# A transformer block on one core: charges and router tokens turned by way of memory, second statistics on ScalarE, a new order

## The chip, the cores and the metric

The kernel runs on one core of a Trainium2 chip. The metric is the device time of one execution in microseconds. A core has five engines that run side by side, each through its own instructions in a fixed order: TensorE (PE; its weight loads are PEld), VectorE (DVE), ScalarE (ACT), GpSimd (POOL) and SyncE (SP), which here issues nearly all transfers between memory (DRAM) and the on-chip buffer (SBUF). TensorE writes its results to PSUM, eight banks of 128 x 512 numbers.

## What is computed

The input x has 32 sequences of 512 tokens with 256 numbers each, all in float32. The reference adds two blocks to it:

```python
x = x + attn(layernorm(x))
x = x + ffn(layernorm(x))
# attn, per sequence
q = tanh(x @ W_charge.T + b_charge)[..., 0]            # one number per token
shell = normalise(x @ W_shell.T + b_shell)             # 64
proj = shell @ omega.T + rff_bias
phi_s = concat([cos(proj), sin(proj)]) * rff_scale     # 64
phi = (mags * q**[0..4] outer phi_s) @ W_combine.T     # 64
attn = softmax(causal(phi @ phi.T * decay / temp))
out = (attn @ (x @ W_v.T + b_v)) @ W_out.T + b_out
# ffn, per sequence
h = gelu([x, mean of slots] @ w1.T + b1)               # 128
alpha = softmax over the 8 largest of (h @ w2.T + b2) / (|tau| + 0.1)   # 64 slots
slots = GRU(alpha.T @ x / sum(alpha), slots)
out = (alpha @ (slots @ wv.T + bv)) @ wo.T + bo
```

## The kernel before, in words

Two sequences form a group (`GB = 2`, 1024 tokens, eight tiles of 128 tokens); 16 groups follow each other, and several are in work at once. A group goes through these stages; names are those of the tiles in the profile:

1. Load: `x` (token by partition), and, from the third group on, `xb`, the same numbers loaded a second time from DRAM in blocks of 32 x 32, so that VectorE's 32 x 32 transposes (L876) give `xT`, the tokens turned so that the feature is the partition. The first two groups turn on TensorE instead (L854). `xb` has two buffers.
2. First statistics (`bna`, L786, `lna` on POOL), and `pf = xT @ [W_shell, W_charge, W_v W_out]` (L906); VectorE scales it and adds the bias into `sv` (L919).
3. Charges: POOL repeats each token's charge 64 times (`qrep`, L945), TensorE turns this (`ptq`, L965), ScalarE takes tanh and the square into `qs` (L975, L983). Beside it the shells are normalised (`sq`, `rn`, `shn`), turned and projected (`pts`, `pp`); angles are rounded (`turn`), and a sine gives `tp`'s first power. VectorE makes the four others by two products with `qs` (L1099).
4. `pph` combines the powers to `phi` (L1111, L1126).
5. Attention in three pieces per sequence: logits `pl` (L1165), mask and row minimum `lg`, `nm` (L1194, VectorE), exponentials `pr` (L1206, ScalarE), turned on TensorE and copied (`ptp`, L1243; `prT`, L1261), values `po` (L1249), and the residual addition into `x` (L1278, VectorE).
6. Second statistics: `bnb` (L786, VectorE), ten small operations on POOL (`lnb`, L797 to L807), and `xm`, the normalised tokens (L1301, ScalarE). TensorE turns them (`ptb`, L822), ScalarE copies them to `xmT` (L834).
7. Router: `ph` (L1328), gelu `h_t`, `prr`, turned to `prt`, `rl`; the eight largest by `top` and `rest` (L1384, L1385), weights `al` (L1418, POOL).
8. Slots: `psi` (L1442), copied to `gi` (L1456, VectorE), GRU (`prz`, `pn`, `rz`, `nn`, `rh`, `hn`), values `pv`, outputs `py` (L1600), added to `x` (L1614, VectorE) and stored by SP (L1619).

The order of each engine's instructions is worked out by a planner in the file when the program is built (`Plan.order`). Each step is added with its engine, a cost, the steps it needs, the tiles it uses and, for a transfer, a time to landing. The planner places the step that can start first, ties going to the lower rank; a rank is the group's number times `STRIDE` plus the step's place in its group plus a `DELAY` of its stage. It also knows how many buffers each kind of tile has (`SLOTS_OF`) and holds a step back until one is free. An engine then carries out its list strictly in order: an instruction that waits holds up all behind it, on SP too.

Of the kernel before, what the change touches and what calls it, by code (L numbers as in the profile page):

```python
# [11 lines left out]
AF = mybir.ActivationFunctionType  # L12
# [12 lines left out]
BY_TENSOR = 2  # L25
SHELL = 64
# [30 lines left out]
    "xT": 4,  # L57
    "xmT": 4,
# [9 lines left out]
    "row": 7,  # L68
    "half": 4,
# [3 lines left out]
HOP = 0.41  # L73
TABLE = 1.28
SWITCH = 1.77
STRIDE = 26.98
LATE = 0.0
# [3 lines left out]
    "load": (4.9, -6.0),  # L81
    "tokens": (10.7, 1.0),
    "angles": (-1.4, -34.3),
    "phi": (3.9, 0.9),
    "weights": (-3.0, 1.9),
    "values": (17.8, -4.4),
    "normal": (17.2, 16.3),
    "router": (34.1, 12.7),
    "taken": (-19.4, 7.1),
    "gru": (-29.8, 4.8),  # L90
    "given": (20.5, 17.4),
# [152 lines left out]
def block_kernel(ctx: ExitStack, tc: tile.TileContext, a: dict, out: bass.AP):  # L244
# [11 lines left out]
    def lazy(tag, name, shape, dtype=F32):  # L256

        if tag not in pools:
            kind = {"space": bass.MemoryType.PSUM} if tag == "ps" else {}
            pools[tag] = ctx.enter_context(  # L260
                tc.tile_pool(name=f"{tag}_pool", bufs=SLOTS_OF.setdefault(tag, 1), **kind)
            )
        return Lazy(tag, lambda: pools[tag].tile(shape, dtype, tag=tag, name=name))
# [87 lines left out]
    w1x = const("w1x", [P, KD, H])  # L351
    b1e = const("b1e", [H, 1])
# [324 lines left out]
    l_w1x = load("SP", w1x, rows(a["w1_t"][0:D, :]), 128, rank=30.0)  # L677
    l_w1s = load("SP", w1s, rows(a["w1_t"][D : 2 * D, :]), 128, rank=30.0)
# [99 lines left out]
    def statistics(g, n, src, uses, after):  # L778

        st = small(f"bn{n}_{g}", [P, GT, 6])  # L780
        ts = small(f"ln{n}_{g}", [P, 5, GT])
# [11 lines left out]
        def spread():  # L793

            mean, rs, dm, va, nmr = (ts()[:, k, :] for k in range(5))
# [8 lines left out]
            if n == "b":  # L804
                ev.tensor_tensor(mean, st_[:, :, 1], st_[:, :, 4], ALU.add)
                ev.tensor_tensor(nmr, mean, rs, ALU.mult)
                ev.tensor_scalar(nmr, nmr, -0.5, None, ALU.mult)  # L807

        s = add("POOL", 3.3 if n == "a" else 4.1, spread, ss + [s_ones], [st, ts])
        return ts, s  # L810

    def transposed(g, n, src, uses, after, tag):

        res = {}
        for bb in range(GB):
            for k in range(KD):
                pt = bank(f"pt{n}_{g}_{bb}_{k}")
                dst = lazy(tag, f"{tag}_{g}_{bb}_{k}", [P, T])

                def turn(bb=bb, k=k, pt=pt):  # L820
                    for c in range(NT):
                        nc.tensor.transpose(  # L822
                            pt()[:, c * P : (c + 1) * P],
                            src()[:, bb * NT + c, k * P : (k + 1) * P],
                            ident,
                        )

                s = add(
                    "PE", 0.47, turn, after[bb * NT : (bb + 1) * NT] + [s_ident], uses + [pt, dst]
                )  # L830
                s = add(
                    "ACT",
                    0.54,
                    lambda dst=dst, pt=pt: nc.scalar.copy(dst(), pt()),  # L834
                    [s],
                    [pt, dst],
                )
                res[bb, k] = (dst, s)
        return res
# [49 lines left out]
    def features(g):  # L889
# [6 lines left out]
        ln, s_ln = statistics(g, "a", xt, [xt], arrived)  # L896
# [41 lines left out]
        qrep = lazy("row", f"qrep_{g}", [P, GB, NT // 2, 2, PHI_S])  # L938
# [3 lines left out]
        def repeated(bb):  # L942
            for h in range(2):
                lo = bb * NT + (h ^ bb) * (NT // 2)
                nc.gpsimd.tensor_copy(  # L945
                    qrep()[:, bb, :, h, :],
                    sv()[:, lo : lo + NT // 2, C_Q : C_Q + 1].to_broadcast([P, NT // 2, PHI_S]),
                )

        s_rep = [  # L950
            add(
                "POOL",
                0.63,
                lambda bb=bb: repeated(bb),
                s_sv[bb * NT : (bb + 1) * NT],
                [qrep, sv],
            )
            for bb in range(GB)
        ]
        ptq = bank(f"ptq_{g}")  # L960
        qs = lazy("qs", f"qs_{g}", [P, 2, T])

        def charges_turned():
            for c in range(NT):
                nc.tensor.transpose(  # L965
                    ptq()[:, c * P : (c + 1) * P],
                    qrep()[:, c // 2, c % 2].rearrange("p h s -> p (h s)"),
                    ident,
                )

        s = add("PE", 0.45, charges_turned, s_rep + [s_ident], [qrep, ptq, qs])
        s = add(
            "ACT",
            0.61,
            lambda: nc.scalar.activation(qs()[:, 0, :], ptq(), AF.Tanh),  # L975
            [s],
            [ptq, qs],
            "exp",
        )
        s_q = add(  # L980
            "ACT",
            0.62,
            lambda: nc.scalar.activation(qs()[:, 1, :], qs()[:, 0, :], AF.Square),  # L983
            [s],
            [qs],
        )

# [23 lines left out]
        def norms():  # L1011
# [7 lines left out]
                0.4,  # L1019
# [72 lines left out]
        for m in (1, 3):  # L1092

            def powers(m=m):
# [612 lines left out]
```

## Time and profile before

| | |
|---|---|
| three runs, median (lowest to highest) | 717.17 us (716.65 to 717.93) |
| profiled execution, its own time | 716.61 us |
| span from first to last instruction | 714.8 us |
| busy: PE, DVE, ACT, POOL | 686.8, 595.3, 422.5, 236.2 us |
| mean granted TensorE clock | 0.993 of full speed |
| moved by DMA | 53.76 MB, 75 GB/s over the span |

How to read the rows: a group of instructions has its line, engine, operation, the tiles written and read, shapes and count; then the busy time of all (overlaps once) and the mean duration of one in ns; then the time for which the engine stood idle just before them and who ended it. Rows of stages give the start and end of a stretch, its length, and for PE, PEld, DVE, ACT and POOL the busy time with the number of instructions, then the granted clock, the share of the 16 DMA engines in use and GB/s. A timeline row gives start, duration, engine and operation; SPq is SP's queue, where the duration of several issues is that of the whole series. A landing is the time from the issue of a transfer to the arrival of its last byte.

### The profile page before, as it was taken

The page shows a single profiled execution, that of the slowest core. Times are in us where ns is not written, and L with a number is a line of the kernel's source. Part 1 is how long each engine was busy: PE and PEld are TensorE (multiplying, and loading weights), DVE is VectorE, ACT ScalarE, POOL GpSimd, SP SyncE. Part 2 cuts the span into 40 slices and gives each one's busy share as a digit, 9 for nine tenths or more (in the row PEclk, how much of TensorE's full clock was granted, in tenths as well). Part 3 has the DMA queues.
Part 4 walks back from the last instruction along what each step waited for, and adds up shares of the span by engine and source line. Part 5 has one row for each costly group of instructions (what it writes and reads, how often), then busy time and mean ns, then how long its engine had stood idle before and what let it go on. Part 6 is the DMA issues. An engine that isn't in the chain of part 4 may idle for free.

```text
span 714.8 us, 12300 instructions
## 1 busy us (share of the span) xinstructions
PE 686.8 (96%) x4170; PEld 480.2 (67%) x4170; DVE 595.3 (83%) x1750; ACT 422.5 (59%) x867; POOL 236.2 (33%) x470
## 2 busy tenths in 40 slices
PE   3989999999999999999999999999999999999884
PEld 3757676767676766767676776767667676777453
DVE  3999888789798989979897979979899887878474
ACT  1445849585755747656565856467475655758720
POOL 3640532214334432324324133423423243321120
PEclk9999999999999999999999999999999999999989
DMA  6796113032304223331412333131330301001013
GB/s 179 161 278 121 34 26 60 2 118 58 119 2 115 63 60 118 60 120 25 94 59 60 119 60 118 27 93 60 59 118 1 118 1 60 1 1 60 0 60 118
DMA packets 100016, 53.76 MB, mean 75 GB/s; under 512 B 64017, under 2 KB 99153, under 8 KB 99953
## 3 DMA queue, kind: packets, MB, share of 16 engines
q1 hardware_dynamic: 98640, 52.45, 28.3%
q8 instruction: 33, 0.54, 0.3%
q10 hardware_dynamic: 1104, 0.36, 0.2%
q0 software_dynamic: 208, 0.17, 0.2%
q14 instruction: 31, 0.25, 0.1%
HBM read 35.85 MB, written 16.78 MB: 74 GB/s over the span
## 4 chain that ended last, share of the span: by engine, by line
PE 89%; DVE 4%; ACT 2%; DMA 2%; issue 1%; POOL 1%; DVEq 0%; ACTq 0%; POOLq 0%
PE po L1249 20%; PE pf L906 18%; PE ph L1328 7%; PE pl L1165 5%; PE pph L1111 5%; PE ptp L1243 5%; PE psi L1442 4%; PE py L1600 4%; PE ptb L822 4%; PE prz L1492 4%; PE pv L1580 2%; PE prr L1353 2%; PE pn L1492 2%; PE pta L1563 1%; DMA x<-in_x_dram 1%; PE pp L1053 1%
## 5 line engine op out<-in xcount | busy, mean ns | idle before, releaser
L1249 PE MATMUL po<-sv,prT 128*128 128x256 f32 x640 | 149.6, 380 | 0.0
L906 PE MATMUL pf<-wfb,xT 128*128 128x321 f32 x448 | 133.2, 439 | 0.0
L1249 PEld LDWEIGHTS po<-sv,prT 128*128 128x128 f32 x640 | 117.0, 189 | 22.6 <-issue 5.9
L906 PEld LDWEIGHTS pf<-wfb,xT 128*128 128x128 f32 x448 | 80.4, 190 | 37.5 <-issue 6.8
L1301 ACT ACTIVATE xm<-x,lnb 128x256 f32<-128x256 f32 x128 | 66.0, 594 | 43.3 <-POOL lnb L807 43.3
L1206 ACT ACTIVATE pr<-lg,nm 128x128 f32<-128x128 f32 (+3 forms) x128 | 70.7, 555 | 13.1 <-DVE nm L1194 9.8
L1278 DVE SCALAR_TENSOR_TENSOR x<-po,den,x 128x256 f32<-128x256 f32 x128 | 60.3, 475 | 20.3 <-PE po L1249 20.0
L945 POOL COPY qrep<-sv 128x128 f32<-128x128 f32 x64 | 17.8, 294 | 154.1 <-DVE sv L919 154.1
L919 DVE SCALAR_TENSOR_TENSOR sv<-pf,lna,bias_f 128x321 f32<-128x321 f32 x128 | 63.8, 543 | 4.3 <-PE pf L906 3.9
L1194 DVE CUSTOM_DVE_ANT_0 lg<-pl,mask 128x128 f32<-128x128 f32 (+3 forms) x128 | 55.9, 487 | 6.9 <-PE pl L1165 6.8
L1328 PE MATMUL ph<-xmT,w1x 128*128 128x512 f32 x128 | 59.5, 596 | 0.0
L786 DVE BATCH_NORM_STATS2 bnb<-x 128x6 f32<-128x256 f32 x128 | 53.3, 424 | 3.1
L1261 ACT COPY prT<-ptp 128x384 f32<-128x384 f32 (+1 forms) x96 | 45.9, 517 | 4.9 <-PE ptp L1243 4.7
L786 DVE BATCH_NORM_STATS2 bna<-x 128x6 f32<-128x256 f32 x128 | 46.9, 413 | 0.0
L1243 PE MATMUL ptp<-ident,pr 128*128 128x128 f32 x320 | 45.4, 274 | 0.4 <-ACT pr L1206 0.3
L1243 PEld LDWEIGHTS ptp<-ident,pr 128*128 128x128 f32 x320 | 37.1, 140 | 8.5 <-ACT pr L1206 2.4
L1614 DVE TENSOR_TENSOR x<-py,x 128x512 f32<-128x512 f32 x64 | 39.9, 684 | 3.3 <-PE py L1600 3.0
L834 ACT COPY xmT<-ptb 128x512 f32<-128x512 f32 x64 | 33.3, 589 | 15.8 <-PE ptb L822 15.8
L1165 PE MATMUL pl<-phi 64*128 64x256 f32 (+1 forms) x384 | 42.4, 356 | 0.0
L797 POOL TENSOR_TENSOR lnb<-bnb 128x8 f32<-128x8 f32 x16 | 9.8, 612 | 94.4 <-DVE bnb L786 94.4
L1099 DVE TENSOR_TENSOR tp<-tp,qs 128x1024 f32<-128x1024 f32 x32 | 39.4, 1231 | 1.3 <-ACT tp L1085 0.7
L876 DVE STREAM_TRANSPOSE xT<-xb 128x512 f32<-128x512 f32 x56 | 38.2, 695 | 0.5 <-issue 0.4
(171 smaller groups left out, 1291.7 us busy)
## 6 DMA issues: line engine op xcount, KB each, us to landing
x<-in_x_dram SPq DMA_DIRECT2D x32, 512.0 KB, 4.8
out_dram<-x SPq DMA_DIRECT2D x64, 256.0 KB, 2.5
xb<-in_x_dram SPq DMA_DIRECT2D x112, 128.0 KB, 3.4
setup<-in_gru_whh_t_dram SPq DMA_DIRECT2D x1, 768.0 KB, 4.6
wih<-in_gru_wih_t_dram SPq DMA_DIRECT2D x1, 768.0 KB, 7.9
wfb<-wf SPq DMA_DIRECT2D x8, 40.1 KB, 3.4
setup<-in_W_v_dram SPq DMA_DIRECT2D x1, 256.0 KB, 3.5
setup<-in_W_out_t_dram ACTq DMA_DIRECT2D x1, 256.0 KB, 9.2
```

The source lines that it names most:

```text
L786: lambda t=t: nc.vector.bn_stats(st()[:, t, :], src()[:, t, :]),
L906: nc.tensor.matmul(pf()[:, 0:NF], tile_()[:, k, c * P : (c + 1) * P], w[:, k, :], start=(k == 0), stop=(k == KD - 1),)
L919: lambda t=t, pf=pf: nc.vector.scalar_tensor_tensor(sv()[:, t, :], pf()[:, 0:NF], ln()[:, 1, t : t + 1], bias_f, ALU.mult, ALU.add,),
L1165: nc.tensor.matmul(pls[bb]()[:, off[i] + lo : off[i] + lo + w], phi()[r, 0, q : q + P], phi()[r, 1, k : k + w], start=True, stop=True,)
L1194: nc.vector.tensor_tensor_reduce(out=lg()[:, c], in0=pls[bb]()[:, c], in1=mask[:, T - w : T], scale=1.0, scalar=TOP, op0=ALU.add, op1=ALU.min,
L1206: nc.scalar.activation(pr()[:, c], lg()[:, c], AF.Exp, bias=nm(), scale=-1.0, accum_out=den()[:, tiles.index(i), bb : bb + 1],)
L1243: nc.tensor.transpose(pt()[:, j : j + P], prs[bb]()[:, j : j + P], ident)
L1249: nc.tensor.matmul(po()[:, d * D : (d + 1) * D], pr_t()[:, lo : lo + P], sv()[:, bb * NT + j, C_V:NF], start=(j == 0), stop=(j == i),)
L1261: lambda width=width, pt=pt, pr_t=pr_t: nc.scalar.copy(pr_t()[:, 0:width], pt()[:, 0:width]),
L1278: nc.vector.scalar_tensor_tensor(xt()[:, t, :], po()[:, d * D : (d + 1) * D], den()[:, d, bb : bb + 1], xt()[:, t, :], ALU.mult, ALU.add,)
L1301: lambda t=t: nc.scalar.activation(xm()[:, t, 0:D], xt()[:, t, :], AF.Identity, bias=ln()[:, 4, t : t + 1], scale=ln()[:, 1, t : t + 1],),
L1328: nc.tensor.matmul(ph(), w1x[:, k, :], tiles[k](), start=(k == 0), stop=(k == KD - 1))
```

## The change

Four things are edited at once, and the planner's constants with them, so that the order of all engines is another.

- Charges: ScalarE takes tanh and square on the 128 x 8 charges as they stand in `sv` (`qc`), SP stores these 128 x 16 numbers to a DRAM tile `qd` in the order of the tokens, and four transfers read them back, each repeated over 64 partitions, as `qs`. The copies on POOL and the turns on TensorE go.
- Router's tokens: for all groups but the last two (`LAST_BY_TENSOR = 2`), `xm` is stored to a DRAM tile `xd` (one transfer a sequence), read back in blocks of 32 x 32 by four transfers into a buffer of the kind `xb`, which keeps two buffers, and turned by two VectorE transposes a sequence. The matching rows of `w1` are loaded in that order (`w1b`).
- Second statistics: VectorE's residual addition also sums each row; POOL makes the negative mean; ScalarE squares `x` minus mean with a running sum; POOL makes the scale and shift by three operations.
- The copy of the taken tokens (`gi`) goes from VectorE to ScalarE.

```diff
-    "xT": 4,
-    "xmT": 4,
+    "xT": 3,
+    "xmT": 2,
+    "xd": 2,
...
+    "qd": 2,
-    "row": 7,
-    "half": 4,
+    "row": 6,
+    "half": 5,
-HOP = 0.41
+HOP = 0.35
-SWITCH = 1.77
-STRIDE = 26.98
-LATE = 0.0
+SWITCH = 0.45
+STRIDE = 22.33
+LATE = 1.0
 DELAY = {
...
@@ def normalised(g, xm, after):
+            if g >= NG - LAST_BY_TENSOR:
...
+            else:
+                xd = lazy("xd", f"xd_{g}_{bb}", [T, D])
+                xb = lazy("xb", f"xmb_{g}_{bb}", [P, T // SQ, KD * SQ])
                 s = add(
+                    "SP",
+                    1.0,
+                    lambda bb=bb, xd=xd: nc.sync.dma_start(
+                        out=xd().rearrange("(c p) d -> p c d", p=P),
+                        in_=xm()[:, bb * NT : (bb + 1) * NT, 0:D],
+                    ),
+                    of,
+                    [xm, xd],
+                    land=3.8,
+                )
+                for q in range(P // SQ):
+                    def back(q=q, xd=xd, xb=xb):
+                        nc.sync.dma_start(
+                            out=xb()[q * SQ : (q + 1) * SQ, :, :],
+                            in_=xd().rearrange("(t i) (q e) -> q i t e", i=SQ, q=P // SQ)[q],
+                        )
+                    s_b.append(add("SP", 0.7, back, [s], [xd, xb], land=4.0))
+                for h in range(2):
+                    def turn(h=h, n=n, dst=dst, xb=xb):
+                        nc.vector.transpose(
...
+                    done.append(add("DVE", 0.63, turn, s_b, [xb, dst]))
@@ def features(g):
+        s = add("ACT", 0.25,
+            lambda: nc.scalar.activation(qc()[:, 0, :], sv()[:, :, C_Q], AF.Tanh), s_sv, [sv, qc], "exp")
+        s = add("ACT", 0.2,
+            lambda: nc.scalar.activation(qc()[:, 1, :], qc()[:, 0, :], AF.Square), [s], [qc])
+        s = add("SP", 0.6,
+            lambda: nc.sync.dma_start(
+                out=qd().rearrange("m b (c p) -> p (m b c)", p=P),
+                in_=qc().rearrange("p m t -> p (m t)"),
+            ), [s], [qc, qd], land=3.5)
+        for h in range(2):
+            for bb in range(GB):
+                def repeated(h=h, bb=bb):
+                    lo = (h ^ bb) * HT
+                    nc.sync.dma_start(
+                        out=qs()[h * PHI_S : (h + 1) * PHI_S, :, bb, :],
+                        in_=qd()[:, bb, lo : lo + HT].partition_broadcast(PHI_S),
+                    )
+                s_q.append(add("SP", 0.6, repeated, [s], [qd, qs], land=3.0))
...
-            s_tp.append(add("DVE", 1.25, powers, [s_tp[-1], s_q], [tp, qs]))
+            s_tp.append(add("DVE", 1.25, powers, [s_tp[-1]] + s_q, [tp, qs]))
@@ def attention(g, sv, s_sv, phi, s_phi):
                             ALU.add,
+                            accum_out=ln()[:, 0, bb, i : i + 1],
@@ def router(g, s_x, ln):
-        ln, s_ln = statistics(g, "b", xt, [xt], s_x)
+        for tiles in ((0, 1), (2,), (3,)):
+            s = add("POOL", 0.25,
+                lambda c=c: nc.gpsimd.tensor_scalar(
+                    ln()[:, 2, :, c], ln()[:, 0, :, c], -1.0 / D, None, ALU.mult), ...)
+            for bb in range(GB):
+                for i in tiles:
+                    s_sq.append(add("ACT", 0.6,
+                            lambda bb=bb, i=i: nc.scalar.activation(
+                                xm()[:, bb * NT + i, 0:D],
+                                xt()[:, bb * NT + i, :],
+                                AF.Square,
+                                bias=ln()[:, 2, bb, i : i + 1],
+                                accum_out=ln()[:, 3, bb, i : i + 1],
+                            ), [s], [xm, xt, ln]))
+        def deviations():
+            nc.gpsimd.tensor_scalar(va, va, 1.0 / D, LN_EPS, ALU.mult, ALU.add)
+            nc.gpsimd.tensor_tensor(rs, va, nhalf, ALU.pow)
+            nc.gpsimd.tensor_tensor(nmr, nm, rs, ALU.mult)
...
-        xm_t = transposed(g, "b", xm, [xm], s_xm, "xmT")
+        xm_t = normalised(g, xm, s_xm)
+        w1, w1_done = (w1x, [l_w1x]) if g >= NG - LAST_BY_TENSOR else (w1b, l_w1b)
@@ def slots(g, xm, al, s_al):
-            "DVE", 0.38, lambda: nc.vector.tensor_copy(gi(), psi()[:, 0:D]), [s_psi], [psi, gi]
+            "ACT", 0.38, lambda: nc.scalar.copy(gi(), psi()[:, 0:D]), [s_psi], [psi, gi]
```

## The prediction

> **What bounds the kernel now.** I read the busy shares first, then the chain that ended last, then the table of stages over two groups in the middle (one group in its two alternating orders), then the costliest groups and the waits.
>
> ```profile
> PE 686.8 (96%) x4170; PEld 480.2 (67%) x4170; DVE 595.3 (83%) x1750; ACT 422.5 (59%) x867; POOL 236.2 (33%) x470
> ...
> PE 89%; DVE 4%; ACT 2%; DMA 2%; issue 1%; POOL 1%; DVEq 0%; ACTq 0%; POOLq 0%
> ...
> 350.39:391.56 41.17, 41.17 (x287) 28.68 (x286) 35.46 (x104) 24.93 (x52) 14.78 (x29) 1.00 0.29 78
> 391.56:433.50 41.94, 41.94 (x231) 29.50 (x230) 37.57 (x111) 26.34 (x54) 14.13 (x29) 1.00 0.31 76
> ```
>
> The stage rows give length, then PE, PEld, DVE, ACT and POOL busy. PE has no gap in 83.11 us, so a group takes 41.56 us and PE sets it. DVE is next with 73.03 / 2 = 36.5 us a group; ACT has 25.6. The clock is full (1.00), so no gain or loss hides there. Of the span, 28 us of PE idle lie in the first 58 us and the last 73 us.
>
> **The change part by part.**
>
> *TensorE.* Removed are the turns of the router's tokens (14 of 16 groups; the last two keep them) and the turns of the charges (all 16).
>
> ```profile
> L822 PE MATMUL ptb<-ident,xm 128*128 128x128 f32 x256 | 33.4, 275 | 0.0
> L965 PE MATMUL ptq<-ident,qrep 128*128 128x128 f32 x64 | 9.7, 274 | 0.0
> ```
>
> Busy time counts overlapping matmuls once, so it is the time by which PE's row gets shorter: 33.4 / 16 = 2.09 us a group and 9.7 / 16 = 0.61 us. 14 x 2.09 = 29.2 us; charges count for 15 groups, since group 0's lie in the start where PE waits anyway: 9.1 us. Sum 38.3 us. One rule of the Trainium skill speaks against reading it so: "Perfetto Trace Analysis", Identifying the Most-Contended Engine, holds matmul busy time for a bad measure, since matmuls are pipelined, and takes weight-load share instead, here 67%. If only load time counted, the two loads' rows (28.6 x 14/16 + 7.5 = 32.5 us) would go. But the stage rows show PE without a gap, and four turns advance PE by 0.52 us although each lasts 275 ns; I keep 38.3. A group then needs 41.56 - 2.70 = 38.9 us of PE.
>
> *VectorE.* It loses the second statistics and the copy of the taken tokens, and gains four transposes a group and a running sum in each residual addition.
>
> ```profile
> L1278 DVE SCALAR_TENSOR_TENSOR x<-po,den,x 128x256 f32<-128x256 f32 x128 | 60.3, 475 | 20.3 <-PE po L1249 20.0
> L786 DVE BATCH_NORM_STATS2 bnb<-x 128x6 f32<-128x256 f32 x128 | 53.3, 424 | 3.1
> L876 DVE STREAM_TRANSPOSE xT<-xb 128x512 f32<-128x512 f32 x56 | 38.2, 695 | 0.5 <-issue 0.4
> L1194 DVE DVE_READ_ACCUMULATOR2_ANT nm<- 128x1 f32 x128 | 10.7, 84 | 0.0
> L1456 DVE COPY gi<-psi 128x256 f32<-128x256 f32 x16 | 6.8, 423 | 6.8 <-PE psi L1442 6.4
> ```
>
> A group: -53.3/16 = -3.33; -6.8/16 = -0.42; +4 x 38.2/56 = +2.73 (same shape as the tokens' transposes). The running sum: "VectorE: DVE Perf Modes" (Two Vector instructions with no wait between them) says that an accumulator output makes two instructions; the read in the row of the masked minimum costs 84 ns, so 8 x 0.084 = +0.67 (between 0, if it overlaps the next instruction, and this). Sum -0.35: 36.5 -> 36.15 us a group, now 93% of PE's 38.9 instead of 88%.
>
> *ScalarE.* A group: -33.3/16 = -2.1 (copies of the turned tokens), -(9.7 + 10.2)/16 = -1.2 (charges), +0.45 for two small ones over 128x8 (nearest: 0.2 us each, the 128x1 rows), +8 squares of 128x256 with a sum (the 128x256 exponentials with their reads follow each other every 0.49 us) = +3.9, +0.4 for the taken tokens' copy. 25.6 -> 27.1 us. Not the bound; table loads stay three a group.
>
> *GpSimd.* Ten small operations of the second statistics (rows `lnb`, 72.7/16 = 4.5 us a group) become six, and the charges' copies (17.8/16 = 1.1 us) go. Nobody waits longer for it.
>
> *SyncE and DMA.* SP's queue has 14 transfers a group; 15 come in: two stores of normalised tokens (512 KB), eight loads back (128 KB), one store of charges, four loads that repeat them.
>
> ```profile
> 435.32 2.17 SPq L1619 DMA_DIRECT2D out_dram<-x  x4
> 441.45 0.93 SPq L277 DMA_DIRECT2D x<-in_x_dram  x2
> 461.40 5.85 SPq L277 DMA_DIRECT2D xb<-in_x_dram  x8
> ```
>
> Issue times: 0.54, 0.46 and 0.73 us each. SP's new total is 16 x 0.73 + 11 x 0.54 + 2 x 0.46 = 18.5 us of 38.9: not a bound by throughput. Nor are the DMA engines: 0.30 x 41.56 = 12.5 us a group now; the eight loads back cost as the eight token loads do (58% of 9 us = 5.2 us), stores and repeats (1.5 MB) about as `x` and outputs (7.3 us for 2 MB, so 5.5), charges 2 to 3: some 26 of 38.9 us. Bursts will queue behind each other, which is where latency comes from.
>
> *The new ring.* The order of the changed program's instructions is the same in every middle group. On SP: four token loads, two stores of normalised tokens, three token loads, four loads back (first sequence), the store of charges, one token load, four outputs, three repeats, four loads back (second sequence), the last repeat, `x`. The store of charges stands behind loads that wait until VectorE has emptied the one shared block buffer; the repeats wait for that store to land; the second loads back and the last repeat stand behind them; and VectorE's first product of powers (`tp`, which now waits for all four repeats) stands ahead of all its later work, hence of the transposes that empty the buffer. Once round: VectorE from the first product to the emptied buffer, by pitches in the timeline: six transposes 4.1, second product 1.2, two additions 1.1, eight first statistics 2.9, four `phi` 1.35, five gate operations 2.35, eight masked minima 3.3, eight `sv` 3.9, small ones 0.5 = 20.7 us; then four issues 2.9, charges' issue 0.7, their landing L, three repeats 1.5, four issues 2.9, one repeat 0.5, landing 3.2 (median of the token loads in the middle). Sum 32.4 + L.
>
> L is what no row shows: 2 x 8 numbers from each of 128 partitions, 2048 pieces of 4 bytes written to memory. The skill speaks against it: "DMA: Bandwidth & Descriptors", Rules for kernel authors, says that a non-contiguous last dimension becomes one descriptor per element. Lower end: 2.6 us, the landing of the scalar load `lt` (128 pieces of 4 bytes). Upper end: the charge weights (256 pieces) landed in 3.7; 1.1 us more for 128 pieces, carried on, gives 2.6 + 16.5 = 19.1 us. Nearest row: four token loads, also 2048 pieces: 3 x 0.73 + 3.2 = 5.4 us; behind the loads ahead of it about 1 us more. I take 6.4 us: ring 38.8 us, just PE's 38.9. At L = 9.2 it reaches the 41.56 of now.
>
> *Stalls.* VectorE leaves 38.9 - 36.15 = 2.75 us a group. Its waits for ACT and POOL now (turn 7.2, top 6.0, rh 2.0 and smaller, 19.5 us in all) are 1.2 us a group and stay. New are two waits for loads back and one for repeats, on a queue that is in order. I charge each load 0.95 us (half the spread from 2.4 to 4.3 us of the token loads' landing in the middle), the repeats 0.3, since their ring just closes. 1.2 + 1.9 + 0.3 = 3.4, 0.65 above what is free. While DVE stands there, `sv`, masked minima and additions come late, and PE with them. 14 groups x 0.65 = 9.1 us.
>
> Start and end: group 0's powers need the charges at 43.2 us and have them at 31.6 now; through memory they take some 11 us more, just covered (uncovered 1 to 3 us). In the tail the statistics lose four small POOL operations and get two squares: nothing.
>
> Sum against the profiled execution, 716.6 us (span 714.8 and 1.8 around it): 716.6 - 38.3 + 9.1 = 687.4. The median of the runs lies 0.6 above: 688 us.
>
> **Rivals.**
> - *PE stays without gaps* (landing early enough everywhere, as the DMA engines' free time would allow): 717.2 - 38.3 = 679 us. Against it: 93% of DVE with in-order waits. Chance 0.13.
> - *VectorE or ScalarE sets the pace*: squares stand on ACT between the taken tokens' copy and the exponentials, and the exponentials feed PE. With 1.5 us more a group than forecast, 688 + 14 x 1.5 = 709 us. For it: only 2.75 us free; against: ACT at 70%. Chance 0.15.
> - *The charges' store closes the ring late* (slower): above L = 9.2 us each further us costs 14 us. L = 12: 717.2 + 14 x 2.8 = 756 us; at the upper end 19.1, 717.2 + 14 x 9.9 = 856. For it: 4-byte pieces, 2048 of them, and everything named queued behind; a slow issue of so many pieces would count as part of L. Against: 256 such pieces landed in 3.7. Chance 0.19.
> - *The removed turns were hidden anyway*: no change, 717. Against: PE gapless. Chance 0.03.
>
> **How the numbers follow.** Forecast 688 us (0.50, its own range 680 to 698). The other faster cases add 0.13 and 0.15: faster 0.78. Within 0.2% (1.4 us, about what a measurement of this kernel can tell from no change) 0.03, slower 0.19. The range from 676 to 718 leaves out nearly all of the slower case and a sliver below: 0.2.
>
> **What would show it.** Right: four-turn groups of `xm` only in two groups; PE 648 us busy; DVE about 584; a group of 39 to 40 us with small waits of `xmT` and `tp` for DMA; charges' store landing in 5 to 7 us. Wrong: that store at 10 us or more and `tp` waiting for `qs` in every group (slower); or PE gapless at 38.9 (679); or VectorE's additions well above 475 ns.

## The result, and the profile after

The changed kernel takes 812.32 us (median of four runs, 811.58 to 814.85) against 716.91 us for the kernel before on the same chip: a ratio of 1.133, 95% interval 1.1305 to 1.1363. The forecast was 688 us with a range to 718, so it was wrong in size and in sign. The profiled execution's span is 809.9 us.

From the page of the changed kernel: busy shares, the granted clock in 40 slices, the chain that ended last by engine, four of the costliest groups, and the outputs' row of the transfers.

```profile
PE 696.0 (86%) x3882; PEld 463.8 (57%) x3882; DVE 570.6 (70%) x1790; ACT 444.0 (55%) x1080; POOL 192.1 (24%) x342
...
PEclk9967998899999999999898999989899899989988
...
PE 43%; DMA 24%; DVE 18%; SPq 5%; ACT 4%; issue 3%; POOL 2%; DVEq 0%; ACTq 0%; POOLq 0%
...
L1423 PE MATMUL ph<-xmT,w1b 128*128 128x512 f32 x112 | 69.1, 753 | 43.3 <-DVE xmT L884 38.1
...
L1153 DVE TENSOR_TENSOR tp<-tp,qs 128x1024 f32<-128x1024 f32 x32 | 38.8, 1213 | 49.1 <-DMA qs<-qd 30.4
...
L884 DVE STREAM_TRANSPOSE xmT<-xmb 128x512 f32<-128x512 f32 x56 | 36.4, 688 | 35.4 <-DMA xmb<-xd 35.4
L1335 DVE SCALAR_TENSOR_TENSOR x<-po,den,x 128x256 f32<-128x256 f32 x128 | 55.3, 472 | 7.6 <-PE po L1306 7.6
...
out_dram<-x SPq DMA_DIRECT2D x64, 256.0 KB, 9.3
```

TensorE's share of the chain fell from 89% to 43%; DMA, VectorE and SyncE's queue took it over. The first product of powers `tp` waits 49 us in all, the transposes of the normalised tokens 35 us, and TensorE waits 38 us for those transposes. The outputs, which the change doesn't touch, land in 9.3 us; before it took 2.5. The two stage rows below are one group each (length; PE, PEld, DVE, ACT, POOL busy; granted clock; DMA share; GB/s):

```profile
498.46:545.40 46.94, 42.22 (x238) 27.83 (x237) 35.26 (x111) 26.84 (x67) 11.20 (x21) 0.93 0.58 124
545.40:592.97 47.57, 42.43 (x238) 27.93 (x237) 35.25 (x111) 26.84 (x67) 11.21 (x21) 0.93 0.56 122
```

A group takes 47.3 us; DVE works 35.25 us of it, TensorE 42.3, nobody all of it. So a ring of waits sets the pace. SyncE's part of it is in the timeline of its queue (start, length, line, transfer, how many):

```profile
554.14 1.90 SPq L874 DMA_DIRECT2D xmb<-xd  x4
556.14 0.44 SPq L1020 DMA_DIRECT2D qd<-qc  x1
556.62 1.42 SPq L283 DMA_DIRECT2D xb<-in_x_dram  x1
558.14 2.04 SPq L1712 DMA_DIRECT2D out_dram<-x  x4
567.90 1.89 SPq L1034 DMA_DIRECT2D qs<-qd  x3
569.88 2.42 SPq L874 DMA_DIRECT2D xmb<-xd  x4
572.35 0.58 SPq L1034 DMA_DIRECT2D qs<-qd  x1
```

Its close is in the timelines of VectorE and of TensorE (in brackets: idle before it, and the releaser that the records name):

```profile
576.87 1.22 DVE L1153 TENSOR_TENSOR tp<-tp,qs 128x1024 f32<-128x1024 f32 x1 [6.48 <-DMA x<-in_x_dram]
```

```profile
579.36 3.78 PE L1423 MATMUL ph<-xmT,w1b 128*128 128x512 f32 x4 [5.14 <-DVE xmT L884]
```

The charges' store is issued at 556.14; the first repeat can be issued only at 567.90. Then come the second loads back and the last repeat, and at 576.87, once that has landed, `tp`. (The record names `x`, issued just after the last repeat, as the releaser; `tp` reads no `x`.) The landing of the store in this stretch, from the transfers' table:

```profile
out_dram<-x SPq DMA_DIRECT2D x4, 256.0 KB, 10.9
...
qd<-qc SPq DMA_DIRECT2D x1, 8.0 KB, 11.7
```

Once round the ring, measured, beside the forecast:

| Leg | measured, us | forecast |
|---|---|---|
| VectorE, first product (529.51) to emptied buffer (554.11) | 24.6 | 20.7 |
| four issues, loads back | 2.0 | 2.9 |
| charges' store, issue and landing | 11.8 | 0.7 + 6.4 |
| three repeats, four issues | 4.5 | 4.4 |
| last repeat, issue and landing | 4.5 | 0.5 + 3.2 |
| sum | 47.4 | 38.8 |

The store is 4.7 us over. VectorE's 3.9 us are waits inside its leg: 2.1 for `pph`, 0.6 for `pl`, 0.5 for `prz`, 0.4 for `pf`. The last three stand in the first experiment below too, at full clock and nearly to the same length; only the wait for `pph` differs (the changed kernel first, then the first experiment):

```profile
538.83 0.42 DVE L1180 TENSOR_TENSOR phi<-pph,dec_q 128x256 f32<-128x256 f32 x1 [2.08 <-PE pph L1165]
```

```profile
415.06 0.42 DVE L1180 TENSOR_TENSOR phi<-pph,dec_q 128x256 f32<-128x256 f32 x1 [0.67 <-PE pph L1165]
```

These 1.4 us are TensorE's lateness after its gap, and its clock adds to it. Stretches of the changed kernel's trace, columns as in the stage rows:

```profile
574.20:579.30 5.10, 0.02 (x1) 0.00 (x0) 2.43 (x4) 1.82 (x8) 0.00 (x0) 0.84 0.82 233
579.36:581.00 1.64, 1.64 (x2) 0.84 (x3) 1.61 (x6) 0.00 (x0) 0.00 (x0) 0.50 0.33 76
581.00:583.20 2.20, 2.20 (x5) 0.80 (x3) 2.20 (x10) 0.00 (x0) 0.22 (x1) 0.50 0.81 182
583.20:586.40 3.20, 3.20 (x43) 1.72 (x42) 0.90 (x3) 2.79 (x11) 1.88 (x7) 0.80 0.00 0
586.40:590.00 3.60, 3.60 (x16) 2.19 (x18) 2.65 (x6) 1.44 (x4) 3.00 (x4) 1.00 0.03 7
```

TensorE stood for 5.1 us, and then worked at half clock for some 5 us (all of the stretches at 0.50, and 1.3 us of the one at 0.80): the four `ph` took 3.78 us where four take about 1.9 at full clock. The `pph` that VectorE waits for next comes that much later.

### The profile page after: what moved, and what is told of

Read it like the earlier page. It is cut to its first block, busy times and chain, and to the rows that moved or that the text cites. A ratio compares the mean times of both kernels' runs of the same rounds, so it can differ in the third digit from the quotient of the medians.

```text
span 809.9 us, 12233 instructions
## 1 busy us (share of the span) xinstructions
PE 696.0 (86%) x3882; PEld 463.8 (57%) x3882; DVE 570.6 (70%) x1790; ACT 444.0 (55%) x1080; POOL 192.1 (24%) x342
## 4 chain that ended last, share of the span: by engine, by line
PE 43%; DMA 24%; DVE 18%; SPq 5%; ACT 4%; issue 3%; POOL 2%; DVEq 0%; ACTq 0%; POOLq 0%
PE pf L962 12%; DMA xmb<-xd 7%; DMA qd<-qc 6%; DMA x<-in_x_dram 6%; PE ph L1423 6%; PE pph L1165 4%; PE pl L1222 4%; PE prz L1585 3%; DVE xmT L884 3%; SPq L874 3%; PE po L1306 2%; DMA qs<-qd 2%; PE psi L1535 2%; PE py L1693 2%; DVE x L1707 2%
## 5 line engine op out<-in xcount | busy, mean ns | idle before, releaser
L1423 PE MATMUL ph<-xmT,w1b 128*128 128x512 f32 x112 | 69.1, 753 | 43.3 <-DVE xmT L884 38.1
L1263 ACT ACTIVATE pr<-lg,nm 128x256 f32<-128x256 f32 (+3 forms) x128 | 70.6, 553 | 23.5 <-PE ptp L1300 13.8
L975 DVE SCALAR_TENSOR_TENSOR sv<-pf,lna,bias_f 128x321 f32<-128x321 f32 x128 | 67.2, 543 | 14.1 <-PE pf L962 11.5
L1153 DVE TENSOR_TENSOR tp<-tp,qs 128x1024 f32<-128x1024 f32 x32 | 38.8, 1213 | 49.1 <-DMA qs<-qd 30.4
L1372 ACT ACTIVATE xm<-x,lnb 128x256 f32<-128x256 f32 x128 | 63.5, 501 | 17.7 <-POOL lnb L1360 17.7
L1395 ACT ACTIVATE xm<-x,lnb 128x256 f32<-128x256 f32 x128 | 65.6, 588 | 2.2 <-POOL lnb L1388 2.2
L1423 PEld LDWEIGHTS ph<-xmT,w1b 128*128 128x128 f32 x112 | 24.3, 231 | 67.0 <-DVE xmT L884 35.2
L1165 PE MATMUL pph<-tp,wc 64*64 64x256 f32 x640 | 46.7, 435 | 18.0 <-DVE tp L1153 10.7
L1251 DVE CUSTOM_DVE_ANT_0 lg<-pl,mask 128x256 f32<-128x256 f32 (+3 forms) x128 | 56.4, 484 | 7.1 <-PE pl L1222 6.0
L884 DVE STREAM_TRANSPOSE xmT<-xmb 128x512 f32<-128x512 f32 x56 | 36.4, 688 | 35.4 <-DMA xmb<-xd 35.4
L1360 POOL TENSOR_SCALAR lnb<-lnb 128x2 f32<-128x2 f32 (+1 forms) x48 | 12.8, 268 | 193.5 <-DVE x L1335 191.0
L1511 POOL TENSOR_TENSOR al<-rl,asum 128x512 f32<-128x512 f32 x16 | 16.7, 1042 | 176.9 <-DVE asum L1504 148.3
L1094 ACT COPY shT<-pts 128x512 f32<-128x512 f32 x16 | 9.4, 586 | 70.7 <-PE pts L1089 70.7
```

Source lines behind the costliest of these rows:

```text
L884: nc.vector.transpose(dst()[:, :, h * HT : (h + 1) * HT].rearrange("p k (t i) -> p t k i", i=SQ), xb()[:, h * n : (h + 1) * n, :].rearrang ...
L975: lambda t=t, pf=pf: nc.vector.scalar_tensor_tensor(sv()[:, t, :], pf()[:, 0:NF], ln()[:, 1, t : t + 1], bias_f, ALU.mult, ALU.add,),
L1165: nc.tensor.matmul(phs[h]()[bb * COMB : (bb + 1) * COMB, 0:HT], wc[r, m, :], tp()[r, m, bb * HT : (bb + 1) * HT], start=(m == 0), stop=(m ...
L1251: nc.vector.tensor_tensor_reduce(out=lg()[:, c], in0=pls[bb]()[:, c], in1=mask[:, T - w : T], scale=1.0, scalar=TOP, op0=ALU.add, op1=ALU.min,
L1263: nc.scalar.activation(pr()[:, c], lg()[:, c], AF.Exp, bias=nm(), scale=-1.0, accum_out=den()[:, tiles.index(i), bb : bb + 1],)
L1372: lambda bb=bb, i=i: nc.scalar.activation(xm()[:, bb * NT + i, 0:D], xt()[:, bb * NT + i, :], AF.Square, bias=ln()[:, 2, bb, i : i + 1], a ...
```

## The experiments

All kernels below start from the changed one. Unless it is said otherwise, the order of the other engines' instructions is that of the changed kernel.

### The same store in 64-byte pieces

```diff
-                out=qd().rearrange("m b (c p) -> p (m b c)", p=P),
+                out=qd().rearrange("m b t -> (m b t)").rearrange("(p n) -> p n", p=P),
```

> The changed kernel with its order unchanged, but the store of charges writes each partition's 16 numbers as one piece of 64 bytes (128 pieces) instead of 2048 pieces of 4 bytes. The charges then belong to other tokens: that order is left out, nothing else. Theory A (the 4-byte store lands after 11.7 us and closes the ring through SP's queue late): it lands in about 3 us, outputs again in 2.5 to 3.5, a group takes 39 to 41 us, in all 690 to 712 us. Theory B (the round trip of the router's tokens through the one shared buffer sets the pace): still 780 us or more. Theory C (squares on ScalarE and in-order waits of VectorE set it): still 780 or more.

Measured: 698.27 us, ratio 0.974 (0.9694 to 0.9785) to the kernel before: 114 us less than the changed kernel for one access pattern of an 8 KB store. From its page, the busy shares and the chain; then the stage row of one whole group:

```profile
PE 661.6 (95%) x3882; PEld 451.4 (65%) x3882; DVE 570.8 (82%) x1790; ACT 444.5 (64%) x1080; POOL 198.9 (29%) x342
...
PE 88%; ACT 4%; DVE 2%; DMA 2%; SPq 1%; issue 1%; POOL 0%; ACTq 0%; DVEq 0%
```

```profile
353.10:392.80 39.70, 39.70 (x238) 27.07 (x236) 35.24 (x110) 26.83 (x68) 12.13 (x21) 1.00 0.53 148
```

TensorE is gapless again, at 39.70 us a group and full clock. The store lands in 1.4 to 4.4 us (median 2.6), the outputs in 2.6. So everything that the change loses hangs on how this store is cut up.

### One part of the change at a time, and another landing for the planner

These three keep the 4-byte store (or, in the first, do without it), but the planner orders the instructions anew. The first turns the charges on TensorE as before; the second turns the router's tokens on TensorE in all groups; the third tells the planner a longer landing.

```diff
# first: the charges' copies, turns, tanh and square of the kernel before, in place of qc, qd and the repeats
# second
-LAST_BY_TENSOR = 2
+LAST_BY_TENSOR = 16
# third
-            land=3.5,
+            land=11.5,
```

> The changed kernel with the charges' part alone undone: copies on GpSimd, turns on TensorE, tanh and square on ScalarE as before; the router's tokens still go by way of memory. The planner orders anew. TensorE needs 39.5 us a group. A: 695 to 715 us. B: 780 or more, VectorE waiting for the blocks of the router's tokens in every group. C: 760 or more.

Measured: 728.50 us, ratio 1.0161 (1.0114 to 1.0209). Above the expected range. In the middle its outputs follow each other every (528.12 - 286.45) / 6 = 40.28 us, 0.58 more than in the first experiment, and TensorE is busy for 149.5 of 150 us. The spacing is uneven (39.9 to 40.6 us over other stretches of seven and eight groups), so the price of the charges' turns can't be read from it more closely than 0.2 to 0.9 us. Part of the rest is at the end, where this order leaves TensorE idle for 28 us of the last 177; the first experiment has 18 of the last 147.

> The router's tokens are turned on TensorE in all 16 groups; the charges still go through memory by 4-byte pieces. The planner orders anew. A: the store still lands after 10 us or more and the ring is shorter by the second loads back (2.5 us), about 45 us a group: 750 to 790 us. B: 700 to 720 us (TensorE's 41 us a group). C: 780 or more.

Measured: 801.10 us, ratio 1.1174 (1.106 to 1.1288); a little over what theory A expected. Theory C's "780 or more" fits as well, but the first experiment has spoken against C. SyncE's queue waits, from the profiles of the second (first line) and of the changed kernel (below it):

```profile
SPq L1034 <- DMA qd<-qc: 130.6, 15, 10.8
```

```profile
SPq L1034 <- DMA qd<-qc: 97.9, 13, 10.0
```

(Columns: microseconds in all, times, longest.) The store alone, without the router's tokens by way of memory, costs most of the loss: with the charges through memory the kernel is slow with or without the tokens' part.

> The changed kernel, but the planner is told that the store of charges lands after 11.5 us instead of 3.5 and orders anew: same work, same pieces. If the order alone can take the store out of the ring, 690 to 740 us; if the slow store also holds up outputs and loads behind it on the DMA engines so that no order helps, 770 us or more. A expects something between, about 745; B and C expect 800.

Measured: 851.05 us, ratio 1.1871. Theory A's 745 us is missed; the case "770 us or more" came. The repeats hardly wait for the store now (3.3 us in all), but what is issued behind it is still held up: in one group the four transfers issued from 487.8 to 491.3 us whose landings the records give land after 11.3 to 12.3 us, and VectorE waits 45.5 us in all for router tokens that come back. How much of the loss is this and how much the new order as such can't be told from this run.

### Fewer and larger pieces, same result

VectorE turns the charges' block of 128x32 (two copies of the 16 columns) and four stores of 128-byte pieces go out:

```diff
+        qt = small(f"qt_{g}", [P, SQ])
...
+                nc.vector.transpose(qt(), qc().rearrange("p m r t -> p (m r t)")),
...
+                    out=qd().rearrange("m b (c k i) -> k (m b c) i", k=NT, i=SQ)[k],
+                    in_=qt()[k * SQ : (k + 1) * SQ, :],
```

> The changed kernel in its order, its result kept: VectorE turns the charges' 128 x 32 block once a group (tanh and square each twice, to fill 32 columns), and four transfers of 32 partitions store 128 pieces of 128 bytes where 2048 pieces of 4 bytes were. Theory A (the pieces of 4 bytes are the whole loss): about 698 us, as with pieces of 64 bytes, plus up to 3 for three more issues on SP in the ring: 695 to 706, faster than before. Theory B' (the wrong charges of the earlier run made it look fast): above 750.

Measured: 704.19 us, ratio 0.9809 (0.9774 to 0.9844); the four stores land in 1.7 us (median).

Charge and square lie side by side, so that the store has 1024 pieces of 8 bytes:

```diff
-        qc = small(f"qc_{g}", [P, 2, GT])
-        qd = lazy("qd", f"qd_{g}", [2, GB, T])
+        qc = small(f"qc_{g}", [P, GT, 2])
+        qd = lazy("qd", f"qd_{g}", [GB, T, 2])
...
-                out=qd().rearrange("m b (c p) -> p (m b c)", p=P),
+                out=qd().rearrange("b (c p) m -> p (b c) m", p=P),
```

> The changed kernel in its order, its result kept: charge and square of a token lie side by side in memory, so that the store has 1024 pieces of 8 bytes. If the landing goes by the number of pieces (4.9 ns each after 1.7 us): 6.7 us, ring 42.5 less what the slow clock adds, a group 40 to 42 us, 703 to 735 us. If it goes by a fixed penalty of a store with small pieces: 11 to 12 us as before and 800 to 815 us.

Measured: 702.58 us, ratio 0.9794 (0.9749 to 0.984). The store lands in 4.6 to 7.7 us (median 5.0), the outputs in 4.0.

```profile
out_dram<-x SPq DMA_DIRECT2D x4, 256.0 KB, 3.9
...
qd<-qc SPq DMA_DIRECT2D x1, 8.0 KB, 5.0
```

The fence is the transfers' table of a stretch of 15 us around one store. Half the pieces, and less than half of the 11.7 us: with twice as many pieces, each half as long, the changed kernel's store takes 6.7 us more.

The third step, 512 pieces of 16 bytes, keeps the order in which a partition holds its charges; the repeats then read whole 2 KB stretches and the products read them with a stride:

```diff
-        qd = lazy("qd", f"qd_{g}", [2, GB, T])
+        qd = lazy("qd", f"qd_{g}", [2 * GB, P, 4])
...
-                out=qd().rearrange("m b (c p) -> p (m b c)", p=P),
-                in_=qc().rearrange("p m t -> p (m t)"),
+                out=qd().rearrange("k p i -> p k i"),
+                in_=qc().rearrange("p k m c -> p k (m c)"),
...
+                for k in range(2):
+                    q = qs().rearrange("x b p m c -> x m b c p")[:, k if m == 1 else 1]
+                    a = tp()[:, 0 if m == 1 else 1 + k, :]
+                    nc.vector.tensor_tensor(cut(tp()[:, m + k, :]), cut(a), q, ALU.mult)
```

> The charges keep the order in which a partition holds them: the store goes out as 512 pieces of 16 bytes, dense in 8 KB (two charges and their two squares together), the four repeats read whole 2 KB stretches, and VectorE's products read the repeated charges with a stride (four products over 512 columns in place of two over 1024). Theory A (the store's landing is a price for each piece where the pieces meet in the same few lines of memory, about 4.9 ns each, as 2048 pieces in 11.7 us and 1024 in 5.0 us say): 512 pieces land in 3 to 3.5 us, outputs behind them in under 3.5, TensorE gapless in the middle at 39.7 us a group, 697 to 700 us. Theory B (a strided operand costs VectorE double): the products take 4.9 instead of 2.4 us a group, VectorE is then at 38 of 39.7 us and waits show on TensorE: 705 to 720 us.

Measured: 702.26 us, ratio 0.9795 (0.977 to 0.982). The store lands in 2.6 to 5.4 us (median 3.5), the outputs in 3.3. The products (the instructions on the tile `tp`: shortest, median and longest in ns) cost nearly what Theory B said, 4 x 1.09 = 4.4 us a group for 2 x 1.22 (here a token's charge follows the last one's after 16 bytes; after 8 bytes, in the kernel with pairs, the product kept its 1.22 us):

```profile
L1158 DVE TENSOR_TENSOR tp<-tp,qs x64: 1056/1094/1910, 43.1 to 613.8; 128x512 f32<-128x512 f32 x64
```

```profile
250.00:500.00 250.00, 250.00 (x1499) 168.76 (x1497) 232.07 (x700) 167.65 (x418) 74.19 (x131) 1.00 0.55 144
```

But in the second fence, a stage row over six groups, TensorE still has no gap: VectorE had those 2 us free. The time is 2 us above what Theory A said. The two kernels of 702 us and the one of 704 us are equal within their intervals, and are the fastest of the study that keep the result.

### Where the landing comes from: the same pieces elsewhere

Here the charges go out and come back as in the first experiment, and beside them an extra store sends the same 2048 pieces of 4 bytes to a buffer that nothing computes from. Only their place in memory changes: side by side in 8 KB, or 256 bytes apart in 512 KB.

```diff
+        qx = lazy("qx", f"qx_{g}", [2, GB, T, 1])      # dense
+        qx = lazy("qx", f"qx_{g}", [2, GB, T, 64])     # spread
...
+                nc.sync.dma_start(
+                    out=qx()[:, :, :, 0].rearrange("m b (c p) -> p (m b c)", p=P),
+                    in_=qc().rearrange("p m t -> p (m t)"),
+                ),
```

> The charges that are read back are stored in pieces of 64 bytes (their order left out); beside it each group stores the same 2048 pieces of 4 bytes, side by side in 8 KB, to a place that nobody reads or waits for but the eighth transfer after it. If the wait of the repeats for the landing is what costs: about 700 to 715 us. If the pieces hold up every transfer behind them on the DMA engines (outputs landed in 9 to 11 us instead of 2.5): 760 to 815 us, since the second loads back stand behind them.

> As the run with the side store, but its 2048 pieces of 4 bytes lie 256 bytes apart, in 512 KB. If the write end is slow because the pieces meet in the same few lines of memory: side store lands in 4 to 6 us and the time is 700 to 712 us. If every piece costs its own read and write in memory wherever it lies: it lands in 10 us or more, and the time is that of the dense side store.

Measured: dense 805.66 us (ratio 1.1231), spread 706.58 us (0.985). The outputs stand behind the extra store; their row of the transfers, dense first, spread second:

```profile
out_dram<-x SPq DMA_DIRECT2D x64, 256.0 KB, 9.6
```

```profile
out_dram<-x SPq DMA_DIRECT2D x64, 256.0 KB, 3.7
```

The extra store's own landing, dense:

```profile
DMA to landing us min/median/max: 10.7/11.5/13.2
```

Spread, it lands in 4.0 to 5.4 us (median 4.7). It is the same number of pieces of the same size through the same queue. Nobody reads the extra store, yet the records put 52.6 us of waits before the repeats down to it in the dense kernel (0 in the spread one): the third repeat is the eighth transfer after it, the one that waits for it. So this pair doesn't part waiting for the store from being held up behind it. The outputs, however, are issued well before it has landed, and land at 9.6 us all the same.

Three more places and ways tell what "elsewhere" means: 64 bytes apart in 128 KB; 8 bytes apart with the 16 pieces of one partition side by side, so that a stretch of 64 bytes comes from one partition only; and the dense store issued from ScalarE's queue.

```diff
-        qx = lazy("qx", f"qx_{g}", [2, GB, T, 1])
+        qx = lazy("qx", f"qx_{g}", [2, GB, T, 16])     # 64 bytes apart
+        qx = lazy("qx", f"qx_{g}", [P, 16, 2])         # a partition's pieces together,
+                    out=qx()[:, :, 0],                 #   8 bytes apart
# ScalarE's queue
-                nc.sync.dma_start(
+                nc.scalar.dma_start(
```

> Charges stored as 128 pieces of 64 bytes and read back (their order is left out), beside them the extra store of 2048 pieces of 4 bytes that feeds no computation, its pieces now 64 bytes apart in 128 KB. Theory A (pieces are dear where several share a stretch of 64 bytes): no two share one, so the extra store lands in 4.5 to 5.5 us as at 256 bytes apart, 705 us. Theory B (what counts is the size of the region, or stretches larger than 64 bytes): landing between 6 and 11.5 us and 730 to 800 us.

Measured: 706.69 us, ratio 0.9857 (0.9834 to 0.988). Its extra store lands as the spread one does, as Theory A says:

```profile
DMA to landing us min/median/max: 4.6/5.2/7.3
```

> Charges stored as 128 pieces of 64 bytes and read back (their order is left out), beside them the extra store of 2048 pieces of 4 bytes that feeds no computation; the pieces lie 8 bytes apart in 16 KB, and the 16 of one partition lie side by side, so that a stretch of 64 bytes gets its pieces from one partition, one after another. Theory A (a stretch of memory takes its pieces one at a time, whoever sends them): still dear, landing 8 to 12 us, 770 to 810 us. Theory B (dear is that pieces of different partitions, sent by different DMA engines, meet in one stretch): landing 4 to 6 us, 705 us.

Measured: 814.62 and 827.02 us; the rows are from the second. Theory A: still dear. The outputs' row, and the extra store's landing:

```profile
out_dram<-x SPq DMA_DIRECT2D x64, 256.0 KB, 10.6
```

```profile
DMA to landing us min/median/max: 9.6/12.0/15.6
```

Eight pieces in each 64 bytes, all from one partition, are as dear as sixteen from sixteen partitions. So it isn't that different partitions meet. Pieces 4 and 8 bytes apart, in 8 and 16 KB, are dear; pieces 64 and 256 bytes apart, in 128 and 512 KB, are cheap. That a 64-byte stretch gets several pieces is the reading that fits all four; distances between 8 and 64 bytes were not tried, nor was the size of the region apart from the distance.

> Charges stored as 128 pieces of 64 bytes and read back (their order is left out), beside them the extra dense store of 2048 pieces of 4 bytes that feeds no computation, now issued from ScalarE's queue instead of SyncE's. Theory A (the backlog stands in the DMA engines and in memory, which all queues share): outputs issued behind it still land in 9 to 10 us and the time stays at 780 to 810 us. Theory B (only what is behind it in the same queue is held up): outputs land in 3 us, 700 to 710 us.

Measured: 828.57 us, ratio 1.1557. The time is on Theory A's side, above its range; the outputs' median landing looks like Theory B's. The outputs' row, and SyncE's waits:

```profile
out_dram<-x SPq DMA_DIRECT2D x64, 256.0 KB, 2.8
```

```profile
SPq L1720 <- DMA qx<-qc: 61.0, 6, 10.6
SPq L1023 <- DMA qx<-qc: 44.4, 4, 14.1
```

SyncE's queue itself stood still until the store on ScalarE's queue had landed (156 us over the program, with the smaller rows), and issued most outputs after that. Hence they land fast, and late. What SyncE did issue meanwhile was held up. Transfers issued between 471.6 and 472.6 us, with their landings:

```profile
xb<-in_x_dram SPq DMA_DIRECT2D x1, 128.0 KB, 11.5
qx<-qc ACTq DMA_DIRECT2D x1, 8.0 KB, 11.8
qd<-qc SPq DMA_DIRECT2D x1, 8.0 KB, 11.6
```

The token load and the 64-byte store on SyncE's queue land with the extra store on ScalarE's, although neither waits for it. In the group at 284.6 us three outputs issued 2.3 to 3.5 us after the extra store landed after 10.6 to 10.8 us. So the backlog is shared by both queues, which is Theory A's mechanism.

## Why the prediction was wrong, point by point

**The step that failed** is L, the landing of the charges' store: "I take 6.4 us". It took 11.7 from the issue on (11.6 to 13.2 over the program, median 12.1), inside the stated ends of 2.6 and 19.1, and the rival "The charges' store closes the ring late" was the one that came. The nearest row was chosen by the number of pieces: four token loads, 2048 pieces in 5.4 us. But those are loads that fill the chip's own memory, and their pieces are long. The runs put the cost elsewhere. With the number and size of the pieces kept, the landing goes from 11.5 to 5.2 or 4.7 us if the pieces lie 64 or 256 bytes apart, and the kernel from 806 to 707. In the changed kernel's trace the DMA engines take in the 2048 pieces in less than 1.4 us (2471 packets between 557.2 and 558.6 us filled 112.6% of the 16 engines' time: 10 ns of one engine for each). Then they stand almost idle for three microseconds, and then count as full while little moves. DMA activity of 559 to 562 us and of 562 to 565 us:

```profile
DMA packets 109, 0.03 MB, mean 9 GB/s; under 512 B 109, under 2 KB 109, under 8 KB 109
...
q1 hardware_dynamic: 109, 0.03, 3.8%
```

```profile
DMA packets 586, 0.28 MB, mean 95 GB/s; under 512 B 406, under 2 KB 586, under 8 KB 586
...
q1 hardware_dynamic: 586, 0.28, 101.4%
```

In the second stretch the token load and the outputs behind the store pass, at 95 GB/s with the engines full; the stretch at 574.2 us shown above moves 233 GB/s at 82%. So the engines have taken in the store's pieces early, and what holds up the store and all that follows for nine more microseconds lies behind them, on the writing side. That is an inference from the placement runs and these two stretches; no record shows the memory itself.

The rule that the prediction weighed, "DMA: Bandwidth & Descriptors", Rules for kernel authors, did speak against the change: one descriptor for each element. The count it warns of is right (about 2048 short packets), but the count alone isn't what costs: the spread stores have the same count and cost 8 us in a kernel of 698. The same page's Specifications put the least size for full rate at 512 bytes, below which a transfer reads, modifies and writes; here 64-byte pieces land in 1.4 to 4.4 us and 4-byte pieces 64 bytes apart in 5.2 (median), so being shorter than 512 bytes does not by itself cost ten microseconds either.

**The price above the threshold** was too low as well. "L = 12" was to give 756 us; it gave 812. By the forecast's own ring L of 11.3 (11.7 less the issue) makes 43.7 us a group; it was 47.4. VectorE's leg is 3.9 us over and the last repeat's landing 0.8, while the issues took 1.0 less. The forecast had summed VectorE's pitches and left out its waits for TensorE. Those for `pl`, `prz` and `pf`, 1.5 us, are there at full clock too. That for `pph` comes from TensorE's gap, of which the forecast priced only the length: after a gap of 5.1 us TensorE needs some 2.4 us more (`ph` 1.9, `pph` 0.5), and VectorE's wait grows from the 0.7 us of the first experiment to 2.1, inside the ring, once a group. "TensorE: Matmul & The Clock Gate", What's actually happening, says the like: half clock after an idle window of about 3.4 us, and a busy window as long to come back. This trace agrees that a gap is followed by half clock (0.50 after 5.1 us), for longer, some 5 us of work. By that rule, an estimate, half of 3.4 us comes on top of the rival's 2.8 us a group: 717.2 + 14 x 4.5 = 780 us in place of 756. The half clock's part was read in the trace; no run tried it alone.

**What was right.** The ring itself and its order; that `tp` and the transposes would wait for DMA; that the store at 10 us or more means slower; VectorE's busy time (570.6 us for 584), ScalarE's (26.8 us a group for 27.1), and that GpSimd bounds nothing.

**What came out right for another reason.** With the store out of the way (first experiment) a group takes 39.70 us where the forecast said 38.9 + 0.65 = 39.55. That is luck, two errors that nearly cancel: TensorE has no gap there, so the 0.65 of stalls isn't seen, and the removed turns shortened the group by 41.56 - 39.70 = 1.86 us instead of 2.70. TensorE's busy time fell to 661.6 us, not 648. Half of the shortfall stands in the rows of the kernel before (start, length; each block of turns and what follows it):

```profile
437.68 1.09 PE L822 MATMUL ptb<-ident,xm 128*128 128x128 f32 x8
438.61 1.25 PE L906 MATMUL pf<-wfb,xT 128*128 128x321 f32 x4
439.69 1.03 PE L822 MATMUL ptb<-ident,xm 128*128 128x128 f32 x8
440.66 0.93 PE L1165 MATMUL pl<-phi 64*128 64x128 f32 x8
...
452.40 0.60 PE L965 MATMUL ptq<-ident,qrep 128*128 128x128 f32 x4
452.84 0.38 PE L1466 MATMUL pt_gi<-ident,gi 128*128 128x128 f32 x2
```

The next instruction starts before the last turn's row ends, so busy time counts a block longer than TensorE advances. From start to start these blocks take 0.93 + 0.97 + 0.44 = 2.34 us in this group, and 2.29 on the average of six middle groups (the forecast's "0.52 us" for four turns is 0.47). The weight loads' time, which the forecast weighed and set aside, gives nearly this: (28.6 + 7.5) / 16 = 2.26 us. The other 0.4 us are spread over instructions that advance a little more slowly in the first experiment (start to start, `prz` by 0.12 us a group, `pf`, `pn` and `pt_gi` by 0.09 each); why is open. The running sum's read on VectorE was charged 0.67 us; it lies beside the next instruction (in the changed kernel's timeline two additions start 0.40 us apart, with a read of 0.08 us after the first), so it was the lower end, nothing.

**The start** was not "just covered": in the first experiment TensorE waits 3.9 us at group 0's `pph` for the charges by way of memory, over the "1 to 3" that were named if uncovered.

## What to carry to other kernels

The price of a store that turns a layout by scattering single elements can't be told from its bytes, its issue or the number of its pieces alone; it depends on where the pieces fall. Here 2048 dense 4-byte pieces took 12 us to land and held up what was issued behind them, on another queue too; 64 bytes apart they took 5. Pairing them, or letting a partition keep its own 16 bytes together, took the kernel from 812 to 702 us. When a landing stands inside a ring of waits and no row of the trace has the same kind of write, its upper end should carry more of the chance than the nearest load does. And once a ring gets longer than the busiest engine's work, count the other engines' waits inside it, and the slow clock after TensorE's gap, as parts of the ring.

## What the runs showed of the hardware

- Pieces of 4 bytes to memory, 2048 of them, median landings: 11.5 to 12.1 us dense in 8 KB, 12.0 at 8 bytes apart, 5.2 at 64 bytes apart, 4.7 at 256 bytes apart. Dense pieces of 8 bytes: 5.0 us for 1024; of 16 bytes: 3.5 for 512; of 64 bytes: 2.6 for 128.
- What is issued behind a dense store is held up with it. In the same queue: outputs at 9.3 to 10.6 us in place of 2.6. From another queue: a token load at 11.5 us and a 64-byte store at 11.6.
- TensorE after a gap of 5.1 us: granted clock 0.50 for some 5 us of its work.
- VectorE's product of 512 columns took 1.09 us with one operand read in steps of 16 bytes (half of the 1.22 us for 1024 contiguous ones would be 0.61); in steps of 8 bytes 1024 columns kept 1.22 us.
